# First batch's queries as seven block products, with the sums around them moved between engines

## The chip, the cores and the metric

The kernel runs on one core of one Trainium2 chip. The time is device microseconds from start to end of one execution; lower is better. Engines are named as in the profile: PE is TensorE (PEld its weight loads), DVE is VectorE, ACT is ScalarE, POOL is GpSimd, SP is SyncE, which only issues DMAs here.

## What is computed

Hidden states of 2 batches x 1,024 tokens x 512 are layer-normed to `xn`. Two things are made of `xn`, and the output joins them: single-head attention, and a mixture of 8 experts of which each token uses its best two.

```python
xn = layernorm(x)
q, k, v = split(xn @ w_qkv.T + b_qkv)                       # each (2, 1024, 512)
s = softmax(q @ k.T / sqrt(512)) @ v @ w_out.T + b_out
logits = xn @ router_w + router_b                           # 8 experts
w, idx = softmax(top_k(logits, 2))
h_e = silu(xn @ expert_w[e] + expert_b[e])
f = sum over the two experts of w * h_e
y = xn + f @ proj_w + proj_b
out = x + s * silu(norm_w * y / rms(y))
```

All data are float32.

## The kernel before, in words

Tokens are in 16 tiles of 128 (`NT`), 8 to a batch; the width of 512 is four chunks of 128 (`KC`). Every matmul of float32 shows as two records of the profile.

**Weights folded.** Wq and Wk are multiplied once into `wqk` (`product`, L583), and Wv and Wout into `rwvo` (`product_vo`, L407), so queries are `xn @ wqk + u` and values are ready to be summed as output. The biases enter through small sums: `weighted` (L320) is a weighted sum of four chunks of a weight on DVE, and `columns` (L331) turns it with four small matmuls against `ones`. `sq` (from the turned Wq and the bias of K) becomes column 8 of the router's weights `rw`, copied at L487; `sk` (from the turned Wk and the bias of Q) becomes `u`; `vb` (from Wout and the bias of V) is added to `bo` (L531, L532) and later to the values. `turn_w` (L132) turns Wq or Wk, four transposes on DVE.

**The order is that of the program.** `keep_order` (L71) ties every engine's instructions to the written order. So an instruction that waits holds all behind it on its engine; the same goes for the DMAs that an engine issues (SP, POOL and ACT issue DMAs here).

**First stage (L420 to L544).** For each tile, `parts` (L340, four `bn_stats` on DVE), `means` and `variances` (L353 and L368, for 2 or 4 tiles at once: a small matmul `pmean` or `pvar` on PE, then small instructions on DVE, among them three that write `dev` and one that writes `shift`, and a root on ACT), `norm` (L377, on ACT), `store` (L385, SP writes `xn` to DRAM), `turn_x` (L393, one transpose on DVE into `xnT`), and `value_half` (L457, PE: half of the tile's values and, in half 0, the router's logits). The loop over tiles t = 2 to 15 (L500) has these calls in a hand-made order: a tile's turn one step ahead of its product, its norm two ahead, means and variances of tiles 4, 8 and 12 at t = 2, 5 and 9. Between them stand: `bo`'s load on POOL (t = 2, L519), the turn of Wk (t = 8), `sk` (t = 9), `vb` (t = 10), `u` (t = 11), `pvb` (t = 12), which is the last user of the pool `raw`, and the 32 loads of the experts' weights `ew` into that pool's memory (t = 13, L535 to L542), half issued by SP, half by POOL. `eb`, the experts' biases (2 MB, L548), follows on SP.

**Routing and queries (L550 to L754).** DVE finds each token's experts and its place in a list sorted by expert, some 40 small instructions in a chain. PE needs its results at `pk` (L640), at the matmuls of `ptok` (L712, which take `lsel` and `tsel`) and at `pm` (L746). Between these PE does `product(0)` to `product(3)` and the first batch's queries: `queries(oc)` (L550), for each of four chunks of the outcome 2 halves x 4 chunks of the sum = 8 matmuls of 512 columns into a pair of banks (`ps_big`, two buffers), then one instruction of ACT adds `u` and writes `qT`. The memory of `qT` is that of the turned Wq and Wk, `wqkT`, until `product(3)` has read it.

**Experts (L757 to L867).** Tokens go by in `NS` = 39 slots of 128 rows. In a pipeline (L846), the slot's rows are fetched by an indirect DMA of POOL seven slots ahead (`gather`), written and read back in another order by SP (`put_s`, `take_s`), turned on DVE one slot ahead (`turn_s`), multiplied by the expert's weights on PE (`expert`, `ph`), given `eb` by DVE (L840) and SiLU by ACT, and written to DRAM. `pw` (the projection) is loaded at slot 8.

**Attention, combination, gate (L879 on).** The second half of the kernel works on pairs of tiles. It has block products by seven already: scores and attended values of pairs are made from seven products of half blocks with sums on DVE and POOL (`pair_scores`, `attend`).

Of the kernel before, what the change touches and what calls it, by code (L numbers as in the profile page):

```python
# [20 lines left out]
P = 128  # L21
# [6 lines left out]
def kernel(  # L28
# [200 lines left out]
    for q in range(4):  # L229
        for j in range(KC):  # L230
            gps.tensor_copy(bqk[ts(q, QP), :, j], bqkv[ts(j, QP), 0:2, q])  # L231
    spread(gps, wZ[0], w_qkvT[:, ts(0, H)], others)
# [6 lines left out]
    ln_eps = const.tile([P, 1], FP, name="ln_eps")  # L239
    gps.memset(ln_eps, LN_EPS)  # L240
    rms_eps = const.tile([P, 1], FP, name="rms_eps")
    gps.memset(rms_eps, RMS_EPS)
# [3 lines left out]
    ones = const.tile([P, P], FP, name="ones")  # L246
    gps.memset(ones, 1.0)

# [71 lines left out]
    def weighted(w_, bias, name):  # L320

        s_ = raw.tile([P, H], FP, tag="s", name=name, bufs=3)
        for c in range(KC):
            b_ = bias[:, c : c + 1]
            if c:
                dve.scalar_tensor_tensor(s_, w_[:, c, :], b_, s_, ALU.mult, ALU.add)
            else:
                dve.tensor_scalar(s_, w_[:, c, :], b_, None, ALU.mult)
            yield s_
# [120 lines left out]
    sum_q = weighted(wqkT[:, 0:KC], bqk[:, 1], "sq")  # L450
    next(sum_q)
    next(sum_q)
# [23 lines left out]
    value_half(0, 1)  # L476
    means(2, 2)
    next(sum_q)
    sq_ = next(sum_q)
    value_half(1, 1)  # L480
# [3 lines left out]
    pbb = ps_mm.tile([P, 512], FP, tag="mm", name="pbb")  # L484
    pe.matmul(pbb[:, 0:KC], lhsT=ones, rhs=bb, start=True, stop=True)
    dve.tensor_reduce(rb[:, E:E1], pbb[:, 0:KC], AX.X, ALU.add)
    dve.tensor_copy(rw[:, :, E], columns(sq_, "pw"))  # L487
# [12 lines left out]
    for t in range(2, NT):  # L500
# [14 lines left out]
        if 3 <= t < 7:  # L515
            parts(2 * t + 2)
            parts(2 * t + 3)
        if t == 2:
            gps.dma_start(bo, b_out.partition_broadcast(P))  # L519
        if t == 8:  # L520
            turn_w(wqkT[:, KC:], wZ[1])
        if t == 9:
            *_, sk_ = weighted(wqkT[:, KC:], bqk[:, 0], "sk")
        if t == 10:

            *_, vb = weighted(wo, bqkv[:, 2], "vb")
        if t == 11:
            dve.tensor_copy(u, columns(sk_, "pu"))
        if t == 12:
            pvb = ps_mm.tile([P, 512], FP, tag="mm", name="pvb")  # L530
            pe.matmul(pvb, lhsT=ones, rhs=vb, start=True, stop=True)  # L531
            dve.tensor_tensor(bo, pvb, bo, ALU.add)  # L532
            close(raw_guard)
        if t == 13:
            ew_guard, ewp = pool("ew", side="right")  # L535
            ew = ewp.tile([P, E, KC, H], FP, name="ew")
            for e in range(E):
                for q in range(4):
                    (sp if q in ours else gps).dma_start(  # L539
                        ew[ts(q, QP), e],  # L540
# [212 lines left out]
    for oc in range(2, KC):  # L753
        queries(oc)  # L754
# [608 lines left out]
```

## Time and profile before

| what | value |
|---|---|
| median of 3 runs | 541.28 us (538.69 to 543.67) |
| the profiled execution | 540.82 us |
| its span in the profile | 539.1 us |
| PE busy | 527.3 us (98%) |
| DVE busy | 311.2 us (58%) |
| POOL busy | 236.0 us (44%) |
| ACT busy | 167.0 us (31%) |
| first stage, PE's values from L487 on | from 32.0 us |
| queries of the first batch (L555) | from 105.6 us |
| first expert slot on PE | 134.5 us |
| first scores of attention on PE (L1057) | 256.1 us |

The profile is of one execution. Its page has the busy time of each engine, the span in 40 slices (the clock that PE was granted is one row), the chain of work that ended last, the costliest groups of instructions, and the DMA issues. A group's line gives line, engine, operation, what is written and read, and the count; then busy time in us and the mean of one in ns; then how long the engine sat idle before these and what ended it. A timeline's line gives start and length in us, engine, line, operation, count, and in brackets the idle time before it and its releaser. Where several like instructions follow each other they are merged, and the length is that of all.

### The profile page before, as it was taken

The page shows a single profiled execution, that of the slowest core. Times are in us where ns is not written, and L with a number is a line of the kernel's source. Part 1 is how long each engine was busy: PE and PEld are TensorE (multiplying, and loading weights), DVE is VectorE, ACT ScalarE, POOL GpSimd, SP SyncE. Part 2 cuts the span into 40 slices and gives each one's busy share as a digit, 9 for nine tenths or more (in the row PEclk, how much of TensorE's full clock was granted, in tenths as well). Part 3 has the DMA queues.
Part 4 walks back from the last instruction along what each step waited for, and adds up shares of the span by engine and source line. Part 5 has one row for each costly group of instructions (what it writes and reads, how often), then busy time and mean ns, then how long its engine had stood idle before and what let it go on. Part 6 is the DMA issues. An engine that isn't in the chain of part 4 may idle for free.

```text
span 539.1 us, 5950 instructions
## 1 busy us (share of the span) xinstructions
PE 527.3 (98%) x1762; PEld 322.1 (60%) x1762; DVE 311.2 (58%) x565; ACT 167.0 (31%) x316; POOL 236.0 (44%) x272
## 2 busy tenths in 40 slices
PE   7999999999999999999999999999999999999996
PEld 5778877444444444444466656756846657484585
DVE  2565652840333333333859376375697685949586
ACT  1535562211311111111333422423426234152340
POOL 8610006022234875230227445246189755464542
PEclk9989999999999999999999999999999999999999
DMA  9995339999999999994387922723625638295512
GB/s 212 206 220 127 78 79 227 275 217 336 319 338 331 359 348 338 318 290 146 125 281 234 299 83 92 273 78 123 229 78 179 230 95 297 71 312 176 187 54 78
DMA packets 89057, 112.37 MB, mean 208 GB/s; under 512 B 6849, under 2 KB 59201, under 8 KB 88897
## 3 DMA queue, kind: packets, MB, share of 16 engines
q1 hardware_dynamic: 75072, 75.51, 47.5%
q0 software_dynamic: 8192, 26.24, 16.4%
q10 hardware_dynamic: 5760, 10.23, 5.0%
q8 instruction: 15, 0.25, 0.2%
q14 instruction: 18, 0.14, 0.1%
HBM read 70.54 MB, written 41.42 MB: 208 GB/s over the span
## 4 chain that ended last, share of the span: by engine, by line
PE 87%; DVE 6%; issue 3%; DMA 2%; POOL 1%; ACT 1%; DVEq 0%; POOLq 0%
PE ph L814 20%; PE so L1147 17%; PE pp L1076 14%; PE po L1013 10%; PE pv L462 10%; PE pq L555 5%; PE pr L574 4%; PE sc L1057 3%; PE pqk L586 3%; DMA wZ<-in_L_attn_w_qkv_dram 2%; DVE sc L1082 1%; DVE pT L120 1%; ACT x L380 1%; POOL bqk L231 1%; DVE h L840 1%
## 5 line engine op out<-in xcount | busy, mean ns | idle before, releaser
L814 PE MATMUL ph<-ew,gT 128*128 x280 | 120.3, 592 | 0.0
L814 PEld LDWEIGHTS ph<-ew,gT 128*128 128x128 f32 x280 | 53.2, 190 | 66.9 <-issue 66.9
L788 POOL DMA_INDIRECT xg<-xn_d,tok x39 | 37.3, 957 | 78.2 <-DMA xs<-xg 52.2
L840 DVE TENSOR_TENSOR h<-ph,eb 128x512 f32<-128x512 f32 x39 | 26.8, 690 | 75.6 <-issue 40.4
L462 PE MATMUL pv<-rwvo,xnT 128*128 128x256 f32 (+1 forms) x256 | 60.9, 394 | 1.8 <-DVE xnT L120 1.0
L462 PEld LDWEIGHTS pv<-rwvo,xnT 128*128 128x128 f32 x256 | 48.6, 194 | 11.2 <-ACT x L380 1.4
L843 ACT ACTIVATE h<-h 128x512 f32<-128x512 f32 x39 | 24.5, 629 | 97.7 <-DVE h L840 89.0
L1013 PE MATMUL po<-pw,ct 128*128 128x512 f32 x112 | 49.2, 592 | 0.0
L975 POOL DMA_INDIRECT hg<-ho_d,posi_m x32 | 32.4, 1013 | 37.0 <-DVE nm L1041 23.4
L1044 ACT ACTIVATE pr<-sc,nm 128x1024 f32<-128x1024 f32 x16 | 18.3, 1145 | 90.7 <-DVE nm L1041 89.0
L1154 DVE TENSOR_TENSOR o<-so,o 128x256 f32<-128x256 f32 x49 | 20.0, 421 | 38.8 <-PE so L1147 25.9
L1192 POOL TENSOR_TENSOR o<-o,base 128x512 f32<-128x512 f32 x14 | 20.6, 1493 | 45.3 <-DVE o L1157 45.3
L1076 PE MATMUL pp<-xnT,qT 128*128 128x512 f32 x84 | 39.5, 592 | 0.0
L1147 PE MATMUL so<-vo,pT 128*128 128x256 f32 x168 | 38.5, 379 | 0.0
L1013 PEld LDWEIGHTS po<-pw,ct 128*128 128x128 f32 x112 | 21.3, 190 | 25.5 <-issue 25.3
L1147 PEld LDWEIGHTS so<-vo,pT 128*128 128x128 f32 x168 | 31.9, 190 | 7.3 <-issue 2.6
L120 DVE STREAM_TRANSPOSE gT<-sz 128x512 f32<-128x512 f32 x39 | 27.4, 702 | 13.4 <-DMA sz<-xs 13.4
L1082 DVE TENSOR_TENSOR sc<-pp,sc 128x512 f32<-128x512 f32 x49 | 31.6, 679 | 5.2 <-PE pp L1076 5.2
L539 POOL DMA_DIRECT2D ew<-in_L_ffn_expert_w_dram x16 | 8.7, 551 | 57.6 <-PE pvb L531 51.2
L574 PE MATMUL pr<-xnT,wqk 128*128 128x256 f32 x128 | 28.8, 381 | 0.9 <-DVE sc L1082 0.9
L120 DVE STREAM_TRANSPOSE pT<-pz 128x1024 f32<-128x1024 f32 x14 | 28.2, 2011 | 0.2 <-DMA pz<-ps 0.2
L574 PEld LDWEIGHTS pr<-xnT,wqk 128*128 128x128 f32 x128 | 24.2, 190 | 6.6 <-DVE sc L1082 2.2
(227 smaller groups left out, 819.9 us busy)
## 6 DMA issues: line engine op xcount, KB each, us to landing
xs<-xg SPq DMA_DIRECT2D x39, 256.0 KB, 4.7
sz<-xs SPq DMA_DIRECT2D x39, 256.0 KB, 4.6
ho_d<-h ACTq DMA_DIRECT2D x39, 256.0 KB, 4.7
ps<-pr SPq DMA_DIRECT2D x16, 512.0 KB, 3.3
pz<-ps SPq DMA_DIRECT2D x16, 512.0 KB, 5.7
xn_d<-x SPq DMA_DIRECT2D x32, 128.0 KB, 2.4
ew<-in_L_ffn_expert_w_dram POOLq DMA_DIRECT2D x16, 256.0 KB, 10.9
ew<-in_L_ffn_expert_w_dram SPq DMA_DIRECT2D x16, 256.0 KB, 13.6
```

The costliest lines, as they stand in the source:

```text
L120: dve.transpose(dst.rearrange(f"p j {order} -> p i j a", a=QP), z.rearrange("p i (j b) -> p i j b", b=QP),)
L462: pe.matmul(pvs[t][:, n, : HH + E1 * (1 - n)], lhsT=xnT[t // ST][:, c, ts(t % ST, P)], rhs=rwvo[:, c, cols], start=(c == 0), stop=(c == KC ...
L555: pe.matmul(ps[:, half, :], lhsT=wqk[:, c, ts(oc, P)], rhs=xnT[0][:, c, ts(half, 512)], start=(c == 0), stop=(c == KC - 1),)
L574: pe.matmul(ps[:, :PW], lhsT=wqk[:, c, ts(oc, P)], rhs=xnT[1][:, c, ts(k, PW)], start=(c == 0), stop=(c == KC - 1),)
L788: gps.indirect_dma_start(out=xg[s], out_offset=None, in_=xn_d, in_offset=bass.IndirectOffsetOnAxis(ap=tok[:, s : s + 1], axis=0),)
L814: pe.matmul(ph, lhsT=g_[:, c, :], rhs=ew[:, ds(r, 1), c, :].rearrange("p e f -> p (e f)"), start=(c == 0), stop=(c == KC - 1),)
L840: dve.tensor_tensor(h, ph, eb[:, ds(r, 1), :].rearrange("p e f -> p (e f)"), ALU.add)
L975: gps.indirect_dma_start(out=g_, out_offset=None, in_=ho_d, in_offset=bass.IndirectOffsetOnAxis(ap=posi_m[:, n, t : t + 1], axis=0),)
L1013: pe.matmul(po, lhsT=c_[:, c, :], rhs=pw[:, c, :], start=(c == 0), stop=(c == KC - 1))
L1076: pe.matmul(ps, lhsT=l_[:, c, :], rhs=r_[:, c, :], start=(c == 0), stop=(c == KH - 1))
L1082: dve.tensor_tensor(dst, ps, other, ALU.add)
L1147: pe.matmul(ps[:, :w_], lhsT=l_[:, c, :], rhs=r_[:, c, :], start=(c == 0), stop=(c == SK - 1),)
```

## The change

- Three memsets on POOL (`ln_eps`, `rms_eps`, `ones`) stand before the loads of Wq.
- `weighted` takes an engine and does all four chunks at once. `sq` stays on DVE and is finished before the first values. `sk` and `vb` go to POOL, where a chunk after the first is two instructions (a scaling into `m_`, a sum): seven in all each.
- `value_half(1, 1)` stands before `means(2, 2)`; `pbb` and the copy into `rw` before `variances(2, 2)`.
- In the loop: `parts` of tiles 12 and 13 at t = 6 and of 14 and 15 at t = 7 (before: 5 and 6); `vb` at t = 2 on POOL, after `bo`'s load; `pvb` at t = 4; Wk's turn and `sk` at t = 5; `u` and the end of `raw` at t = 8; the weights of expert e at t = 8 + e.
- The first batch's queries are `wqk` (2 x 2 blocks of 256 x 256) times `xnT[0]` (2 x 2 blocks of 256 x 512) by seven block products with 4 sums of each side's blocks. S1 to S4, of `wqk`, are made on DVE; T1 to T4, of `xnT[0]`, on POOL, T1 in the place of the outcome's block C22. The sums live in a new pool `qs`. The products' sums are made on DVE from PSUM, two instructions of 512 columns for each; `u` is added on the way. Products 1 and 4 stand before `ptok`, 6 after the routing, 7, 5 and 3 after `pm`. Product 2 stands at slot 0 of the experts; ACT copies it to `pw`'s memory and POOL adds it to C11.
- `eb` is loaded after `qs` has been closed, into its place, issued by ACT.

The core of the diff:

```diff
-    def weighted(w_, bias, name):
+    def weighted(w_, bias, name, eng):
         s_ = raw.tile([P, H], FP, tag="s", name=name, bufs=3)
         for c in range(KC):
             b_ = bias[:, c : c + 1]
             if c:
-                dve.scalar_tensor_tensor(s_, w_[:, c, :], b_, s_, ALU.mult, ALU.add)
+                if eng is dve:
+                    dve.scalar_tensor_tensor(s_, w_[:, c, :], b_, s_, ALU.mult, ALU.add)
+                else:
+                    m_ = raw.tile([P, H], FP, tag="m", name=f"{name}_m{c}", bufs=2)
+                    eng.tensor_scalar(m_, w_[:, c, :], b_, None, ALU.mult)
+                    eng.tensor_tensor(s_, s_, m_, ALU.add)
             else:
-                dve.tensor_scalar(s_, w_[:, c, :], b_, None, ALU.mult)
-            yield s_
+                eng.tensor_scalar(s_, w_[:, c, :], b_, None, ALU.mult)
+        return s_
...
-    sum_q = weighted(wqkT[:, 0:KC], bqk[:, 1], "sq")
-    next(sum_q)
-    next(sum_q)
+    sq_ = weighted(wqkT[:, 0:KC], bqk[:, 1], "sq", dve)
...
     value_half(0, 1)
+    value_half(1, 1)
     means(2, 2)
-    next(sum_q)
-    sq_ = next(sum_q)
-    value_half(1, 1)
+    pbb = ps_mm.tile([P, 512], FP, tag="mm", name="pbb")
+    pe.matmul(pbb[:, 0:KC], lhsT=ones, rhs=bb, start=True, stop=True)
+    dve.tensor_copy(rw[:, :, E], columns(sq_, "pw"))
     variances(2, 2)
...
-        if 3 <= t < 7:
-            parts(2 * t + 2)
-            parts(2 * t + 3)
+        if t in (3, 4, 6, 7):
+            first = {3: 8, 4: 10, 6: 12, 7: 14}[t]
+            parts(first)
+            parts(first + 1)
         if t == 2:
             gps.dma_start(bo, b_out.partition_broadcast(P))
-        if t == 8:
-            turn_w(wqkT[:, KC:], wZ[1])
-        if t == 9:
-            *_, sk_ = weighted(wqkT[:, KC:], bqk[:, 0], "sk")
-        if t == 10:
-            *_, vb = weighted(wo, bqkv[:, 2], "vb")
-        if t == 11:
-            dve.tensor_copy(u, columns(sk_, "pu"))
-        if t == 12:
+            vb = weighted(wo, bqkv[:, 2], "vb", gps)
+        if t == 4:
             pvb = ps_mm.tile([P, 512], FP, tag="mm", name="pvb")
             pe.matmul(pvb, lhsT=ones, rhs=vb, start=True, stop=True)
             dve.tensor_tensor(bo, pvb, bo, ALU.add)
+        if t == 5:
+            turn_w(wqkT[:, KC:], wZ[1])
+            sk_ = weighted(wqkT[:, KC:], bqk[:, 0], "sk", gps)
+        if t == 8:
+            dve.tensor_copy(u, columns(sk_, "pu"))
             close(raw_guard)
-        if t == 13:
             ew_guard, ewp = pool("ew", side="right")
             ew = ewp.tile([P, E, KC, H], FP, name="ew")
-            for e in range(E):
...
+        if 0 <= t - 8 < E:
+            e = t - 8
+            for q in range(4):
+                (sp if q in ours else gps).dma_start(
...
-    eb_guard, ebp = pool("eb", side="right")
-    eb = ebp.tile([P, E, H], FP, name="eb")
-    sp.dma_start(eb, expert_b.partition_broadcast(P))
-
-    def queries(oc):
...
+    def times(banks, l_, r_):
+        for o in range(2):
+            for c in range(KH):
+                pe.matmul(
+                    banks[o], lhsT=l_[:, c, ts(o, P)], rhs=r_[:, c],
+                    start=(c == 0), stop=(c == KH - 1),
+                )
+        return banks
...
+    def query_products():
+        p1 = times(big(1), A11, B11)
+        for o in range(2):
+            act.copy(C11[:, o], p1[o].rearrange("p (k f) -> p k f", k=2))
+        p4 = times(mm(4), A22, T4)
+        yield
+        dve.tensor_tensor(S1, A21, A22, ALU.add)
+        dve.tensor_tensor(S2, S1, A11, ALU.subtract)
+        yield
+        dve.tensor_tensor(S3, A11, A21, ALU.subtract)
+        dve.tensor_tensor(S4, A12, S2, ALU.subtract)
+        plus(C12, times(big(6), S2, T2), C11)
+        yield
+        plus(C21, times(big(7), S3, T3), C12)
+        p5 = times(big(5), S1, T1)
+        plus(C22, p5, C21, 1)
+        plus(C12, p5, C12)
+        plus(C21, p4, C21, 1)
+        plus(C12, times(big(3), S4, B22), C12, 0)
+        yield
+
+    def last_query_product(place):
+        p2 = times(big(2), A12, B21)
+        for o in range(2):
+            act.activation(place[:, o], p2[o], AF.Identity, bias=u[:, o : o + 1])
+        gps.tensor_tensor(C11, C11, by_pairs(place), ALU.add)
+
+    gps.tensor_tensor(T3, B22, B12, ALU.subtract)
+    gps.tensor_tensor(T2, T3, B11, ALU.add)
+    gps.tensor_tensor(T4, B21, T2, ALU.subtract)
...
     product(2)
     product(3)
-    queries(0)
+    gps.tensor_tensor(
+        T1, *(b.rearrange("p o (k f) -> p o k f", k=2) for b in (B12, B11)), ALU.subtract
+    )
+    pq = query_products()
+    next(pq)
...
+    next(pq)
     tk = rt.tile([P, 2, NSP], FP, name="tk")
...
-    queries(1)
+    next(pq)
     pm = ps_mm.tile([P, 512], FP, tag="mm", name="pm")
...
-    for oc in range(2, KC):
-        queries(oc)
+    next(pq)
+    close(qs_guard)
+    eb_guard, ebp = pool("eb", side="right")
+    eb = ebp.tile([P, E, H], FP, name="eb")
+    act.dma_start(eb, expert_b.partition_broadcast(P))
...
     for s in range(-steps[0][1], NS):
+        if s == 0:
+            last_query_product(pw[:, 0:2])
         pipeline(steps, s, NS)
```

## The prediction

> **What bounds the kernel now.** I read the page, then the chain of work that ended last, then the timelines of the stages the diff touches, then groups by shape and DMA issues.
>
> ```profile
> span 539.1 us, 5950 instructions
> ...
> PE 527.3 (98%) x1762; PEld 322.1 (60%) x1762; DVE 311.2 (58%) x565; ACT 167.0 (31%) x316; POOL 236.0 (44%) x272
> ...
> PE 87%; DVE 6%; issue 3%; DMA 2%; POOL 1%; ACT 1%; DVEq 0%; POOLq 0%
> ```
>
> TensorE (PE) is busy 98% of the span and 87% of the chain. So an edit counts by what it takes from PE, or by what it makes PE wait for; DVE, ACT and POOL only count where PE waits for them. The chain in order of time (start, length, what) from the queries on:
>
> ```profile
> 105.78 6.87 PE pq L555 x16
> 112.65 1.15 PE ptok L712 x32
> 113.80 6.94 PE pq L555 x16
> 120.74 0.17 PE pm L746 x2
> 120.91 13.79 PE pq L555 x32
> 134.69 109.88 PE ph L814 x256
> ```
>
> Sixteen matmuls of 512 columns take 6.87 us, 0.429 each, back to back through the queries (L555) into the experts (L814): this stretch is priced by counting matmuls. PE's few waits have to be found in the timelines.
>
> **The products (gain).** A logical fp32 product is two records (32 logical in queries, 64 records). Seven block products of 2 x 2 logical are 56 records, so 8 x 0.429 = **-3.43 us**, certain as long as nothing around them waits. Checked from the end of the token matmuls (113.8): p6, then pm, p7, p5, p3, p2 are 3.43 + 0.17 + 4 x 3.43, so ph begins at 131.2 instead of 134.7. DVE has 12 sums from PSUM of 128x512 (L1082 takes 679 ns for one) and four between SBUF tiles (half of L928's 1.22 for 1,024 columns). After p5 ends (124.3) it has eight of them, 5.6 to 6.1 us, then the first turn of gathered rows, 0.70: 131.1 at the latest. p2, placed last and summed by POOL, is the cover: 3.43 us without which ph would wait about 3.4. gT(0)'s data are there: before, gather to turn took 17 us (115.2 to 132.2) beside eb and the last of ew; both are gone from this stretch. S1 and S2 end at 113.2, before DVE needs ptok at 113.8: tok is not late. POOL's C11 sum waits for p2 and delays gather 7 to about 135, whose ph comes at 155: hidden by the 20 us of lead.
>
> **Wk's sums off DVE (gain).** sk and vb (2 x 2.8 us of DVE at L326/L328) leave DVE; before, they stood ahead of a turn that PE waited for (71.81 below): **-0.99**. `pu` and `pvb` only change places on PE; the last `parts` at t = 7 still precede pmean at t = 9.
>
> **The values' bias on POOL (loss).** vb now follows bo's issue on POOL, whose order is fixed. The timeline there:
>
> ```profile
> 28.51 0.18 DVE L357 TENSOR_TENSOR dev<-st,mean 128x16 f32<-128x16 f32 x1
> ...
> 29.39 0.57 POOL L519 DMA_DIRECT2D bo<-in_L_attn_b_out_dram  x1 [0.72 <-DMA x<-_attn_hidden_states_dram]
> ...
> 31.32 0.17 DVE L373 SCALAR_TENSOR_TENSOR shift<-mean,rstd 128x8 f32<-128x8 f32 x1
> ...
> 35.98 1.60 DVE L342 BATCH_NORM_STATS2 st<-x 128x6 f32<-128x128 f32 x8
> ...
> 39.02 0.31 PE L348 MATMUL pmean<-st,eighth 128*128 128x32 f32 x2
> ```
>
> So vb starts at about 30.0 and is seven instructions long. In the changed order DVE does all of sq (ends 29.9), then means(2,2), whose three `dev` instructions read two SBUF tiles, and only then the copy of the router's column for which PE's v(0,0) waits (before: 32.0). The row that decides is from the attention stage (start, length of both, count at the end):
>
> ```profile
> 318.71 2.95 POOL L1006 TENSOR_TENSOR xr<-xr,pb 128x512 f32<-128x512 f32 x2
> ...
> 318.76 3.45 DVE L989 SCALAR_TENSOR_TENSOR hg<-hg,wgt_m,hg 128x512 f32<-128x512 f32 x2
> ```
>
> Alone, L989 takes 743 ns (its minimum); beside two POOL sums two take 3.45, 1.73 each: one full POOL instruction is waited for each time. The Trainium skill, "SBUF — State Buffer", section "Who interferes with whom", says the same and more, that a DVE instruction with two SBUF inputs is blocked entirely while a GpSimd instruction reads SBUF, whatever its length. The row shows this for 512 columns only. By the row alone one could scale the wait with DVE's own length (0.17 x 1.3: four short ones lose 0.9); by the rule each waits out one POOL instruction. I take the rule. POOL's prices:
>
> ```profile
> L965 POOL TENSOR_TENSOR sp<-pT 128x512 f32<-128x512 f32 x7 | 8.9, 1273 | 34.3 <-DVE pT L120 34.3
> ...
> L915 POOL TENSOR_TENSOR sw<-qT 128x256 f32<-128x256 f32 x7 | 5.1, 727 | 6.3 <-DMA xs<-xg 6.3
> ...
> L299 POOL TENSOR_SCALAR mix<-mixed,number 128x128 f32<-128x128 f32 x1 | 0.6, 622 | 0.1
> ```
>
> A sum of 512 columns is 1.27. A scaling (tensor_scalar) is not shown at this width: L299 is 0.62 for 128 columns and L225 0.32 for 32, which continues to 1.81; the skill's "GPSIMD Engine Reference", section "Elementwise — side-by-side cycle accounting", has 769 ns as the best for 512 elements of one input, an estimate of 0.97 with the 0.2 of a 32-column copy (L227). No run here shows that. I take 1.3, between, since L299 compares and L225 is mostly fixed cost. Then dev ends at 30.0 + 1.3 + 1.3 + 1.27 + 3 x 0.2 = 34.5, v(0,0) starts at 34.8; pvar, std, rstd and a blocked `shift` put norm(2) at 36.6 (before 31.5); from there DVE's order is fixed, norm and turn 2.4, two `parts`, turn, two `parts` (1.6, 0.7, 1.6): 42.9, when PE can do pmean of tiles 4 to 7 (before 39.0). **+3.9**. Ends: with no blocking sq's earlier end makes it 38.4, **-0.6**; with scalings of 1.81, +5.6. PE's clock (granted 0.50 from 32 to 35.3 in the windows, after the thin stretch before it) may stay low longer, but PE would then still reach pmean by about 42.3: covered. The earlier ln_eps gives nothing: std gains 1.16, but DVE then waits for wZ until 21.85 all the same.
>
> **Wk turned at t = 5 (loss).** DVE after the variances of tile 8, PE's wait behind sk, and the last instruction ahead of pk:
>
> ```profile
> 53.68 1.64 DVE L342 BATCH_NORM_STATS2 st<-x 128x6 f32<-128x128 f32 x8
> ...
> 55.24 0.69 DVE L120 STREAM_TRANSPOSE xnT<-x 128x512 f32<-128x512 f32 x1
> ...
> 71.81 3.75 PE L462 MATMUL pv<-rwvo,xnT 128*128 128x256 f32 x16 [0.99 <-DVE xnT L120]
> ...
> 97.08 0.29 DVE L636 TENSOR_TENSOR before<-upto,both 128x128 f32<-128x128 f32 x1
> ```
>
> turn_w (2.45) takes the place of 1.64 of `parts`, so tile 7's turn ends at 56.9 where PE wants it at 56.2: **+0.75** (0 to 0.9). Then sk on POOL: 4 x 1.3 + 3 x 1.27 + gaps 0.4 = 9.4 from 56.5 is 65.9, plus the wake, and PE comes to `pu` at 64.75: **+1.3** (0 with scalings of 0.97, +3.6 with 1.81). Behind `pu` on PE stands the whole rest.
>
> **Expert weights from t = 8, and the sums of inputs on POOL (loss).** ew's 32 issues (16 of 0.31 on SP, 16 of 0.55 on POOL) cost PE nothing by themselves: POOL is idle there, and SP's stand between stores that only the gathers at 115 read. But T3, T2, T4 and T1 have 1,024 columns: from 256 to 512 columns 0.55 more, so 2.37 each. T3 waits for the tile x, whose memory qt takes over (by the tiles' sizes in the pools' order), hence for the last store of x, now issued on SP behind expert weights (SP: ew of experts 3 and 4 stand before it). If it lands 2.4 us after its issue as before, the three run at 86 to 93 and DVE's routing (from 92.1, nearly all two-input) is hardly touched. If it waits for the backlog (7.5 MB asked by then in 18 us, some 4.7 delivered at the 260 GB/s of the windows at 84 to 104), it lands at about 93 and all three stand in DVE's way, 7.1 us. The slack: `before` ends at 97.37 and PE reads it at 98.25, 0.88. T1 (after product(3), 105.8) always meets tsel and lsel: 2.37 less the 1.56 that the last lsel is early. So 0.8 + (0 to 6.2): **+3.5**, the middle, one to two of the three in the way.
>
> **Experts' biases later (loss or nothing).**
>
> ```profile
> eb<-in_L_ffn_expert_b_dram SPq DMA_DIRECT2D x1, 2048.0 KB, 15.2
> ```
>
> Now issued by ACT (0.35; behind it p2's copy, not due before 131) once p3 has read qw (127.8), eb must land before h(0) and turn(2) on DVE, which ph(2) needs at 138.0: both take 1.4, so within 8.8 us. Before, it took 15.2 behind 1 MB of ew and beside four gathers, and 2 MB at the 360 to 420 GB/s seen at 120 to 126 would be 5 to 6 and some 2 for latency. Beside puts and takes I expect 10.3: **+1.5** (0 to 5). Behind h(0) on DVE stand the turns, and PE behind these.
>
> **Sum.** -3.43 - 0.99 + 3.9 + 0.75 + 1.3 + 3.5 + 1.5 = +6.5, on the profiled execution's 540.8 (span 539.1 and 1.7 around it): 547.3. The median of the runs lies 0.5 above that execution; **547.5**.
>
> **Rivals.** (1) *The short instructions slip through.* If DVE's instructions of 0.17 to 0.3 us are not held up, the front gives -0.6 in place of +3.9 and the routing 0: -1.5 in all, **539.8**. It speaks for this that the only rows of blocking are of 0.74; against it, that the wait shown there is POOL's length. It decides when `dev` stays at 0.17 to 0.20. (2) *Half of it:* x's last store lands early, or vb starts too late to meet `dev`[...]: 3 to 4 less, **543.5**. (3) *eb is late:* at 200 GB/s, the rate of 112 to 120, 10.5 + 2 and contention make 5, and PE's clock falls in the gap (half of 3.3 us): **553**. (4) *The seven products wait for each other* (DVE's sums hold the two big banks): by the times above p5's bank frees 0.4 before p2 asks; three late sums would give back 2 of the 3.4. It is in the range of all the cases.
>
> **How the numbers follow.** A measurement of this kernel tells about 1% (5.4 us) from no change; its runs spread 0.9%. Forecast 0.45 (544 to 552; 0.38 of it above 546.7, 0.07 below), half 0.25 (0.05 slower, 0.20 same), slipping through 0.22 (with no sk wait and eb hidden 537, and with a front clock that no longer falls 535.3: 0.17 same, 0.05 faster), eb late 0.08 (slower). So faster 0.05, same 0.44, slower 0.51. Range 538.5 to 553.5, leaving out the best of the third and most of the last; the forecast's own is 544 to 552.
>
> **What would show it.** In the new profile: 56 query matmuls and ph starting 17.4 us after ptok; `dev` (L357 to L364) of tiles 2, 3 at a microsecond or more each, v(0,0) near 34.8; PE idle at `pu` before POOL's sk; DVE's routing instructions at 2 us beside T3 to T4; h(0) waiting for eb's DMA. Were `dev` at 0.2 and PE without a gap before pk, the forecast is wrong at its first step.

## The result and the profile after

| | median | runs |
|---|---|---|
| before, measured beside it | 540.42 us | 6, 538.69 to 543.67 |
| changed | 553.74 us | 6, 552.78 to 556.87 |
| ratio | 1.0261 | 95% interval 1.0235 to 1.0287 |

The change costs 13.3 us by the medians. The execution with the profile took 556.74 (span 555.0), one of two of the six that lie 3 us above the other four; what sets these two apart is not settled. Against the profiled span before (539.1) it is 15.9 longer. Four starts on PE, read from the two timelines, show where:

| starts at (us) | before | after | its part of the difference |
|---|---|---|---|
| `product(0)`, behind all values | 91.2 | 96.2 | +5.0 |
| first query product | 105.6 | 110.6 | 0 |
| first expert slot | 134.5 | 143.9 | +4.4 |
| first scores of attention | 255.9 | 271.9 | +6.6 |

From there to the end the two run alike (283.2 and 283.1). PE's waits in the timeline of the changed kernel (start, length, line, in brackets the idle time before and its releaser), where the kernel before, from 41 us to the scores, had only one of 0.99 at 71.81 and one of 0.19 just ahead of the scores:

```profile
57.16 5.05 PE L464 MATMUL pv<-rwvo,xnT 128*128 128x256 f32 x22 [0.70 <-ACT x L384]
...
66.80 1.46 PE L339 MATMUL pu<-ones,sk 128*128 128x1 f32 x8 [2.37 <-POOL sk L330]
...
110.61 3.60 PE L573 MATMUL pq<-xnT,wqk 128*128 128x512 f32 x8
118.42 5.40 PE L573 MATMUL pq<-qt,wqk 128*128 128x512 f32 x8 [4.22 <-POOL qt L628]
...
126.39 3.70 PE L573 MATMUL pq<-qt,qw 128*128 128x512 f32 x8 [0.86 <-DVE qw L606]
...
155.52 4.97 PE L883 MATMUL ph<-ew,gT 128*128 x7 [4.61 <-DVE gT L120]
```

Three things are late: `sk` for `pu`, the third sum of columns (T4) for p4 (the product at 118.42; p1, at 110.61, has no wait), and the rows of slot 2. Behind each of the long waits the clock falls. The stretches of the same trace (times, then busy us of PE, PEld, DVE, ACT, POOL with counts, the granted clock, DMA share, GB/s):

```profile
67.00:74.00 7.00, 7.00 (x23) 5.86 (x23) 1.56 (x6) 0.00 (x0) 4.42 (x8) 0.52 0.68 155
...
118.00:124.00 6.00, 5.58 (x18) 2.50 (x19) 6.00 (x4) 0.00 (x0) 3.65 (x2) 0.72 0.01 3
...
155.00:160.00 5.00, 4.48 (x7) 1.94 (x8) 1.75 (x3) 0.63 (x1) 2.84 (x3) 0.66 1.14 363
```

PE is busy in all 7 us of the first stretch, at half its clock (granted 0.52): the two halves behind `pu` took 3.76 and 3.09 where 1.9 and 2.0 are usual. The wait of 2.37 at `pu`, `pu` itself (1.46, before 0.95) and these 2.9 make +5.8 at this place; with the turn's 0.70, the stall that is gone (-0.99) and a front that is 0.7 sooner, this is 4.8 of the +5.0 in the table. Likewise p4's eight matmuls took 5.40 in place of p1's 3.60. With p4's wait of 4.22 and those at ptok (0.38) and for S2 (0.86) that is 7.3; the table has 7.8, its +4.4 and the 3.43 that the eighth product had taken. Slot 2 waits 4.61 and loses some 2 to the clock (granted 0.66 behind it), the +6.6.

**The sums.** SP's queue (start, length), where the stores of x stand between the weights' loads:

```profile
89.85 6.05 SPq L392 DMA_DIRECT2D xn_d<-x  x4
96.41 3.64 SPq L538 DMA_DIRECT2D ew<-in_L_ffn_expert_w_dram  x4
100.17 1.95 SPq L392 DMA_DIRECT2D xn_d<-x  x4
```

Before, SP issued the last store by 84.5. Here it goes out at 102 and lands at 107.4, as SP's issues are held back by earlier transfers (how, is told at slot 2). T3 starts at once behind it, and meets the widest instructions of the routing. POOL, then DVE:

```profile
107.60 3.67 POOL L626 TENSOR_TENSOR qt<-xnT 128x1024 f32<-128x1024 f32 x1 [23.62 <-DMA xn_d<-x]
```

```profile
109.10 7.07 DVE L752 TENSOR_TENSOR tsel<-hsel,tpart 128x1280 bf16<-128x1280 bf16 x2
116.10 8.91 DVE L769 TENSOR_TENSOR lsel<-mixed,lo 128x1024 bf16<-128x1024 f32 x4
```

The same two on DVE in the kernel before, and a POOL sum of this size with DVE idle in the changed one (C11's):

```profile
104.35 2.90 DVE L691 TENSOR_TENSOR tsel<-hsel,tpart 128x1280 bf16<-128x1280 bf16 x2
107.16 4.62 DVE L704 TENSOR_TENSOR lsel<-mixed,lo 128x1024 bf16<-128x1024 f32 x4
```

```profile
145.49 2.35 POOL L624 TENSOR_TENSOR qT<-qT,pw 128x1024 f32<-128x1024 f32 x1 [5.49 <-ACT pw L623]
```

Both sides lose: a sum takes 3.3 to 3.7 in place of 2.35, `tsel` 7.07 in place of 2.90, `lsel` 8.91 in place of 4.62.

**Slot 2.** SP's waits, and the turn on DVE that PE waits for:

```profile
SPq L116 <- DMA eb<-in_L_ffn_expert_b_dram: 10.3, 1, 10.3
```

```profile
154.75 0.71 DVE L120 STREAM_TRANSPOSE gT<-sz 128x512 f32<-128x512 f32 x1 [3.13 <-DMA sz<-xs]
```

A take of sorted rows (L116) reads nothing of `eb`, yet SP holds it for the 10 us of that load. The built program tells why: the transfers issued by SP and ACT take eight semaphores in turn, and the third take has the one of `eb`, so it may go out only when `eb` has landed. In the same way an issue of SP stands behind the transfer eight before it, which is how the weights' loads hold up the stores.

### The profile page after: what moved, and what is told of

Same layout as the page of the kernel before. It is cut to its first block, busy times and chain, and to the rows that moved or that the text cites. A ratio compares the mean times of both kernels' runs of the same rounds, so it can differ in the third digit from the quotient of the medians.

```text
span 555.0 us, 5967 instructions
## 1 busy us (share of the span) xinstructions
PE 530.5 (96%) x1754; PEld 323.7 (58%) x1754; DVE 325.6 (59%) x573; ACT 165.0 (30%) x316; POOL 272.0 (49%) x291
## 4 chain that ended last, share of the span: by engine, by line
PE 72%; DVE 10%; DMA 10%; issue 3%; POOL 2%; SPq 2%; ACT 1%; DVEq 0%; ACTq 0%; POOLq 0%
PE ph L883 19%; PE so L1217 17%; PE pp L1146 13%; PE po L1083 10%; PE pr L635 4%; PE pv L464 3%; DMA ew<-in_L_ffn_expert_w_dram 3%; DMA wZ<-in_L_attn_w_qkv_dram 3%; PE pq L573 3%; PE sc L1127 2%; DMA eb<-in_L_ffn_expert_b_dram 2%; DVE lsel L769 2%; DVE tsel L752 1%; DMA xn_d<-x 1%; DVE st L346 1%
## 5 line engine op out<-in xcount | busy, mean ns | idle before, releaser
L883 PE MATMUL ph<-ew,gT 128*128 x280 | 122.3, 599 | 4.6 <-DVE gT L120 4.6
L464 PE MATMUL pv<-rwvo,xnT 128*128 128x256 f32 (+1 forms) x256 | 62.1, 399 | 1.9 <-ACT lg L476 1.1
L1114 ACT ACTIVATE pr<-sc,nm 128x1024 f32<-128x1024 f32 x16 | 18.3, 1144 | 90.9 <-DVE nm L1111 89.1
L1083 PEld LDWEIGHTS po<-pw,ct 128*128 128x128 f32 x112 | 21.3, 190 | 25.5 <-issue 25.3
L120 DVE STREAM_TRANSPOSE gT<-sz 128x512 f32<-128x512 f32 x39 | 27.2, 700 | 3.2 <-DMA sz<-xs 3.1
L120 DVE STREAM_TRANSPOSE pT<-pz 128x1024 f32<-128x1024 f32 x14 | 28.1, 2007 | 0.0
L1059 DVE SCALAR_TENSOR_TENSOR hg<-hg,wgt_m,hg 128x512 f32<-128x512 f32 x16 | 24.3, 1554 | 4.4 <-ACT hg L1055 4.4
## 6 DMA issues: line engine op xcount, KB each, us to landing
xn_d<-x SPq DMA_DIRECT2D x32, 128.0 KB, 5.7
ew<-in_L_ffn_expert_w_dram POOLq DMA_DIRECT2D x16, 256.0 KB, 10.3
```

What stands on the lines that cost most here:

```text
L120: dve.transpose(dst.rearrange(f"p j {order} -> p i j a", a=QP), z.rearrange("p i (j b) -> p i j b", b=QP),)
L464: pe.matmul(pvs[t][:, n, : HH + E1 * (1 - n)], lhsT=xnT[t // ST][:, c, ts(t % ST, P)], rhs=rwvo[:, c, cols], start=(c == 0), stop=(c == KC ...
L883: pe.matmul(ph, lhsT=g_[:, c, :], rhs=ew[:, ds(r, 1), c, :].rearrange("p e f -> p (e f)"), start=(c == 0), stop=(c == KC - 1),)
L1083: pe.matmul(po, lhsT=c_[:, c, :], rhs=pw[:, c, :], start=(c == 0), stop=(c == KC - 1))
```

## The experiments

All kernels below are the changed one but for the edit shown, unless said otherwise. The starts on PE are those of one profiled execution each; up to the first it differs by 2 us and more between kernels with the same code there (before 91.2; before without eb 89.1), so the later columns, which are lengths, say more.

| kernel | median | ratio to before | `product(0)` at | to p1 | p1 to slot 0 | slot 0 to scores |
|---|---|---|---|---|---|---|
| before | 540.4 | | 91.2 | 14.4 | 28.9 | 121.4 |
| changed | 553.7 | 1.0235 to 1.0287 | 96.2 | 14.4 | 33.3 | 128.0 |
| e1 weights behind stores | 553.8 | 1.0192 to 1.0286 | 95.7 | 22.4 | 25.5 | 126.5 |
| e2 `u` a step later | 550.4 | 1.0163 to 1.0202 | 88.8 | 14.4 | 33.7 | 128.8 |
| e3 eb issued by POOL | 553.0 | 1.0169 to 1.0255 | 97.1 | 14.4 | 33.2 | 124.8 |
| e4 e1 to e3 together | 546.0 | 1.0087 to 1.0121 | 91.2 | 15.4 | 32.1 | 124.4 |
| e5 sums on DVE, late place | 564.6 | 1.0392 to 1.0470 | 95.3 | 33.5 | 25.5 | 128.5 |
| e6 eb sooner, routing's place | 553.9 | 1.0230 to 1.0291 | 95.0 | 14.4 | 35.4 | 121.5 |
| e7 e1, e2, e5, e6 together | 554.8 | 1.0248 to 1.0300 | 88.9 | 26.1 | 30.4 | 124.5 |
| e8 e7 with eight products | 541.4 | 1.0007 to 1.0035 | 89.1 | 14.4 | 28.9 | 121.4 |
| e9 sums on DVE in its idle time | 549.7 | 1.0108 to 1.0221 | 96.6 | 14.4 | 26.0 | 127.1 |
| e10 eb sooner, sums' place | 552.1 | 1.0176 to 1.0266 | 95.3 | 14.4 | 35.3 | 121.5 |
| e11 e1, e2, e9, e10 together | 540.0 | 0.9981 to 1.0015 | 91.7 | 14.4 | 28.1 | 121.6 |
| e12 e11, sums on POOL | 539.3 | 0.9977 to 1.0007 | 89.8 | 14.4 | 28.9 | 123.2 |
| e13 e11 without eb | 535.3 | 0.9890 to 0.9929 | 88.8 | 14.4 | 25.5 | 121.7 |
| e14 e11, eb ahead of gathers | 539.8 | 0.9984 to 1.0008 | 89.3 | 14.4 | 27.5 | 123.6 |
| e15 e11, weights between stores | 539.4 | 0.9979 to 1.0004 | 89.0 | 14.4 | 28.4 | 121.5 |
| e16 before without eb | 540.5 | 1.0000 to 1.0021 | 89.1 | 14.4 | 28.9 | 121.4 |

### One late thing at a time: e1 to e4

```diff
# e1
-        if 0 <= t - 8 < E:
-            e = t - 8
+        if t == 13:
+            for e in range(E):
# e2 (the weights' loads a step later as well)
-        if t == 8:
+        if t == 9:
             dve.tensor_copy(u, columns(sk_, "pu"))
# e3
-    act.dma_start(eb, expert_b.partition_broadcast(P))
...
         if s == 0:
+            gps.dma_start(eb, expert_b.partition_broadcast(P))
             last_query_product(pw[:, 0:2])
```

> The changed kernel, but the 32 loads of the experts' weights are issued together at t = 13, behind the stores of x, and no longer from t = 8 between them. Theory (the stores of x stand on SP's queue behind the weights' loads, so the sums of columns on POOL start at 107.6 us and TensorE waits 4.2 us for the third of them): the last store lands some 6 us earlier, the wait for the third sum and the low clock behind it go, and about 7.8 us come back: some 546 us. Rival (the sums on POOL and VectorE's selections slow each other down wherever they run together, and the queue has little to do with it): some 2 us come back, 551 us or more.

Measured: 553.8, no gain: the rival's number. The sums did start 10 us sooner, at 97.3, but now among the routing's short instructions. DVE, then PE:

```profile
97.27 2.47 DVE L669 TENSOR_TENSOR key<-lg,m 128x128 f32<-128x128 f32 x1
99.85 2.32 DVE L670 TENSOR_TENSOR key<-key,order 128x128 f32<-128x128 f32 x1
...
102.53 2.07 DVE L675 TENSOR_TENSOR hot<-key,km 128x128 f32<-128x128 f32 x1
```

```profile
107.53 0.59 PE L701 MATMUL pk<-upto,ones 128*128 128x8 f32 x2 [4.84 <-DVE upto L695]
```

Each of these takes 0.29 alone. POOL's three sums (2.35 each) hold one DVE instruction each for nearly their whole length, and the wait moves from p4 to `pk`. The queue was not the cause by itself.

> The changed kernel, but u is taken from pu one step later (t = 9 in place of 8), with the weights' loads one step later too and two experts' loads at t = 15. TensorE should no longer wait 2.4 us for sk. Theory (the last store of x still lands near 107 us, so TensorE only waits longer for the third sum of columns; two waits in a row are not added): about the same, 552 to 554 us. Rival (each wait and the low clock behind it is lost for itself): 5.8 us come back, some 548 us.

Measured: 550.4, 3.3 less. PE no longer waits at `pu`, and `product(0)` starts 7 us sooner in the profile (the medians show half of it; how much clock the wait at `pu` costs differs from run to run, as e5 shows). The last store landed sooner too, near 100, so that p4's wait for T4 stayed as it was (4.61). The number lies between the two theories: the loss at `pu` is at least in part one of its own, since SP and POOL reach the later steps sooner when PE does.

> The changed kernel, but eb's load is issued by POOL and not by ACT, at the start of slot 0. Theory (SP's third take of sorted rows waits for eb's load because the hardware queues' transfers share eight semaphores in turn, and the one that it needs is eb's): the take no longer waits, slot 2's products start where they did before, and some 3 us come back (the wait of 4.6 us, less what VectorE may still wait for eb's data): about 550.6 us. Rival (what counts is only when eb's data land, 10 us after the issue): no change, 553.7 us.

Measured: 553.0, within the scatter of these runs (their intervals overlap). SP's wait for eb is gone, and DVE waits for eb's data in its place:

```profile
153.47 0.69 DVE L908 TENSOR_TENSOR h<-ph,eb 128x512 f32<-128x512 f32 x1 [8.92 <-DMA eb<-in_L_ffn_expert_b_dram]
```

The turns stand behind `h` on DVE, so slot 2 waits 3.10 in place of 4.61. The semaphore is the first of two locks on the same door; the load has to land sooner.

> The three edits together: the weights' loads behind the stores of x, u one step later, eb's load from POOL. Theory: the three losses are those of the order in which loads, sk and eb are issued, and not of the seven products; they come back together, 7.8 + 5.8 + 3.1 us, which gives some 537 us, a little under the kernel before (540.4). Rival (the sums on POOL cost VectorE and TensorE time of their own, whatever the loads do): 543 to 547 us.

Measured: 546.0, 7.8 less than the changed kernel but 5.5 above the kernel before, as the rival said. What is left shows on DVE, where two of the instructions are:

```profile
97.07 2.30 DVE L697 TENSOR_TENSOR before<-upto,both 128x128 f32<-128x128 f32 x1
...
99.48 2.19 DVE L709 TENSOR_SCALAR cnt<-cnt 128x8 int32<-128x8 int32 x1
```

Four instructions of 0.17 to 0.29 take 2.2 to 2.3, one for each of T3, T2, T4 and T1, 8 us of the routing's chain. PE then waits for `lsel` four times (2.8 in all), the clock is at 0.50 from 116 to 122, and slot 2 waits 2.76, as DVE's `h` waits for eb.

### The sums elsewhere: e5 to e8

e5 gives the four sums to DVE, ahead of the sum of the logits, for which it waits 8 us anyway. e6 loads `eb` into the place that the routing leaves, before the seventh product. e7 has both with the edits of e1 and e2; e8 is e7 with `queries(oc)` of the kernel before.

```diff
# e5: x in two tiles, of which the first half is dead by t = 7
+    x_ = [
+        xap.tile([P, ST, 4, P], FP, name="xa"),
+        ln.tile([P, ST, 4, P], FP, name="xb"),
+    ]
...
-    gps.tensor_tensor(T3, B22, B12, ALU.subtract)
-    gps.tensor_tensor(T2, T3, B11, ALU.add)
-    gps.tensor_tensor(T4, B21, T2, ALU.subtract)
+    dve.tensor_tensor(T3, B22, B12, ALU.subtract)
+    dve.tensor_tensor(T2, T3, B11, ALU.add)
+    dve.tensor_tensor(T4, B21, T2, ALU.subtract)
+    dve.tensor_tensor(T1, B12, B11, ALU.subtract)
     dve.tensor_tensor(lg1, lg1, rb.unsqueeze(1).to_broadcast([P, NT, E1]), ALU.add)
# e6: pw and eb on the left, behind close(rc_guard) and before next(pq)
-    eb_guard, ebp = pool("eb", side="right")
+    eb_guard, ebp = pool("eb")
```

> The changed kernel, with the four sums of columns (T1 to T4) made by VectorE in the 8 us in which it waits for the last logits, in a space whose last user is the first half of x (its stores are long done then), and no longer by POOL beside VectorE's routing; u, the weights' loads and eb's load stay as in the changed kernel. Theory (POOL's two-input sums and VectorE's instructions hold each other up, and TensorE waits for the third sum): the wait for the third sum, the wait of ptok and the low clock behind them go, 7.8 us: 546 us; TensorE goes through the queries without a wait. Rival (the loss is the late stores of x): nothing is won, 552 us or more, for the stores are as late as before.

Measured: 564.6, on the rival's side and far above its 552. My layout failed its purpose: `qt` came to lie over the second half of x as well, so DVE stood before its first sum until the last store had landed, and with it the whole routing:

```profile
109.34 1.22 DVE L564 TENSOR_TENSOR qt<-xnT 128x1024 f32<-128x1024 f32 x1 [21.42 <-DMA ew<-in_L_ffn_expert_w_dram]
```

(The releaser named is the transfer that ended last; in the built program the instruction waits for the stores of the second half of x.) It shows the price of the late stores where the waiting engine is not POOL: 16.77 us of PE's waiting at `pk`. And it shows that a sum is 1.22 on DVE.

The run shows one thing more. It has the changed kernel's wait at `pu`, for the same `sk`, and the clock behind it does not fall:

```profile
69.29 1.05 PE L350 MATMUL pu<-ones,sk 128*128 128x1 f32 x8 [2.38 <-POOL sk L341]
```

```profile
69.00:76.00 7.00, 6.71 (x37) 6.01 (x38) 2.17 (x9) 1.41 (x5) 4.65 (x9) 1.00 0.69 155
```

Seven of the profiled executions have this wait (2.37 to 2.39, then the same eight matmuls). Read in windows of half a us, the clock is low for 6.6 to 6.8 us behind it in four of them (changed, e3, e6, e10), for 3.4 in two (e1, e9) and not at all here. So the same wait costs 2.4 to 5.8 us, and one profile shows only one of these prices. The 3 us between the executions of the changed kernel are of this size; that they come from it is not shown.

> The changed kernel, with eb's load issued some 16 us sooner (behind the second batch of query products, in the place that the routing leaves, in front of the seventh product). Theory (both eb's data and the take that shares its semaphore are late by the 10 us that the load takes): the wait of 4.6 us at slot 2 and the low clock behind it go, 6 us: some 547 to 548 us. Rival (POOL's late gathers bound slot 2 anyway): 551 us or more.

Measured: 553.9, no gain in the median, though slot 0 to scores is 121.5 again. Slot 2's wait is gone, but with `eb` in that place the gathers' buffers lie over the sums: the second gather waits for p7 (133.7, 5.8 us behind the first), and PE waits 1.64 for slot 0's rows. The rival's number, by my layout.

> The weights' loads behind the stores of x, u one step later, the sums of columns by VectorE in its idle time and eb's load early. Theory: nothing of the three losses is left, and the gain of seven products (3.4 us) stands with the stall of 1 us that went at t = 10: 536 us, 0.8% under the kernel before. Rival (products that feed each other through VectorE and POOL cannot follow one another without waits): 540 us or more.

Measured: 554.8. Both faults of e5 and e6 in one kernel; POOL's second gather waits for p5 to have read its sums:

```profile
133.97 0.99 POOL L866 DMA_INDIRECT xg<-xn_d,tok  x1 [6.34 <-PE pq L588]
```

> The same as the run with everything mended, but the queries of the first batch by eight products as in the kernel before, without the sums. Theory: 3.4 us above that run (the eighth product), some 539.5 us. Rival (the saved product is lost again in the sums and in waits): no difference to that run.

Measured: 541.4. Not comparable to e7, whose waits come from the sums' space that e8 lacks. It is worth something else: Wk's turn, `vb` and `sk` on POOL and the weights' order, with `u` at t = 9 and no sums, are nearly level with the kernel before (0.2% above it, ratio 1.0007 to 1.0035). So what e7 loses beyond comes with the seven products and their space.

### The layouts mended: e9 to e12

```diff
# e9: the S sums below, the T sums at the top, over the first half of x only; T1 behind S4
+    qw = qs.tile([P, 4, KH, 2 * P], FP, name="qw")
     qt = qs.tile([P, 3, KH, 512], FP, name="qt")
# e10: what p3 and p5 read is put outside eb's place
+    qw14 = qs.tile([P, 2, KH, 2 * P], FP, name="qw14")
+    qw23 = qs.tile([P, 2, KH, 2 * P], FP, name="qw23")
     qt = qs.tile([P, 3, KH, 512], FP, name="qt")
```

> The changed kernel with the sums of columns T3, T2, T4 made by VectorE before the logits' sum, as in the run before, but in a place whose only earlier user is the first half of x, so that they need not wait for the last stores of x; T1 is made by VectorE behind S4. u, the weights' loads and eb's load stay as in the changed kernel. Theory (the late sums and their meeting with VectorE's routing cost 7.8 us, and both go): the sums run at 88 to 93 us, the first products follow each other without a wait, 546 us. Rival (they only lay bare the next wait, the gathers behind the late stores of x): 550 us or more.

Measured: 549.7, 4.0 less. p1 to slot 0 falls from 33.3 to 26.0, and PE's only wait there is 0.36 for S2: the stage's loss is gone, 7.2 us in the profile. The median shows about half and lies near the rival's bound; the waits at other places remain (0.70 for the turn, 2.38 at `pu`, 3.72 at slot 2).

> The changed kernel with the sums' space laid out so that eb's load has to wait for the seventh product (S3, T3) and no longer for the third (S4): it is issued some 7 us sooner. The gathers' space is as in the changed kernel. Theory (eb's data and the semaphore that it shares with SP's third take come too late): slot 2's wait of 4.6 us and the low clock behind it go, 547 to 548 us. Rival: another wait of the slots takes the place, 551 us or more.

Measured: 552.1. Slot 0 to scores is back at 121.5, but slot 0 itself now waits 2.17: eb's load, issued at 132.6, runs while the first rows are fetched (sixth gather at 136.7, seventh at 144.3).

> Both of these, the weights' loads behind the stores of x, and u one step later. Theory: the losses are all gone and one product is saved against the run with eight products (541.4): 538 us. Rival (a wait between the seven products or at the slots remains): 541 us or more.

Measured: 540.0, the kernel before to within 0.2%, and 1.4 under e8 where a product is 3.4. PE passes from p1 to p2 without a wait; the sums sit at 84 to 88 on DVE. Most of the saved product is then lost at the first slot:

```profile
134.18 46.25 PE L894 MATMUL ph<-ew,gT 128*128 x107 [2.45 <-DVE gT L120]
```

> As the run before, but T3, T2 and T4 are made by POOL at the same place. Theory (POOL's sums cost only where VectorE works beside them; here it is idle until 92 us, and they end by then or a little later): within 1.5 us of the run before. Rival (sums on POOL cost in any place): 4 us or more above it.

Measured: 539.3, no different from e11. POOL's sums, 2.35 each, end at 91.2, when one instruction of the routing has begun (held for 0.4). POOL's last sum and that instruction (0.31 in e11):

```profile
88.86 2.35 POOL L567 TENSOR_TENSOR qt<-xnT,qt 128x1024 f32<-128x1024 f32 x1
```

```profile
90.70 0.67 DVE L568 TENSOR_TENSOR lg<-lg,rb 128x144 f32<-128x144 f32 x1 [8.30 <-ACT lg L487]
```

So not the engine but the company was dear: the same three instructions on the same engine held DVE for 6 of e4's 8 us, and for 0.4 here.

### Where the saved product goes: e13 to e16

In e11 the transfers nearly rest from 115 to 117 (DMA share 0.27); eb's 2 MB are issued at 121.5 and take 10.6 us, just when the rows of the first slots go out and come back. SP's waits there:

```profile
SPq L112 <- DMA xg<-xn_d,tok: 20.8, 8, 9.2
...
SPq L116 <- DMA xs<-xg: 6.7, 3, 5.9
```

e13 is e11's kernel and e16 the kernel before, both without the experts' biases: their load is left out and `bo` is added in their place, so the outcome is another one. e14 is e11's kernel with the load placed ahead of the gathers:

```diff
# e13, e16
-    eb = ebp.tile([P, E, H], FP, name="eb")
-    act.dma_start(eb, expert_b.partition_broadcast(P))
...
-            h, ph, eb[:, ds(r, 1), :].rearrange("p e f -> p (e f)"), ALU.add
+            h, ph, bo, ALU.add
# e14: T2 and T4 in pw's place, T3 made a second time, S1 to S4 in lsel's
+            qt = pwp.tile([P, KC, H], FP, tag="pw", name="qt")
...
+    sp.dma_start(eb, expert_b.partition_broadcast(P))
+    qs_guard, qs = pool("qs", side="right")
```

> The mended kernel (sums by VectorE in its idle time) without eb's load: the experts' biases are left out, and b_out's sum bo is added in their place, so that VectorE's instruction stays. Theory (eb's 2 MB beside the first gathers cost slot 0 its 2.5 us): 537 us, 3 us under the mended kernel (540.0). Rival (the chain from the tokens to slot 0 is too long for seven products): 540 us.

Measured: 535.3 (0.989 to 0.993), and slot 0 starts right behind p2:

```profile
128.66 51.53 PE L891 MATMUL ph<-ew,gT 128*128 x119
```

From p1 to slot 0 it is 25.48, 3.43 under the 28.91 of the kernel before: the product, to the last digit. The median is 4.7 under e11's; 2.6 of this is in the stretch from p1 to slot 0, and where the rest lies is not shown.

> The mended kernel with the space laid out anew, so that eb's load is issued right behind the weights' loads and before the first gather, as in the kernel before: T2 and T4 lie in the place of the projection's weights (T3 is made a second time in T4's place, 1.2 us of VectorE), the S sums in the place of lsel. The computation is whole. Theory (as in the run before): slot 0 no longer waits, 537 to 538 us, 0.5% under the kernel before. Rival: 540 us.

Measured: 539.8, the rival's number, though with other waits than the rival's. Slot 0 has no wait, but the stretch from p1 to it is only 0.6 shorter than in e11 (27.5 and 28.1): p6 and p7 wait 0.78 and 0.83 for S2 and for the second T3, which this layout makes late. Two later slots wait 0.86 and 0.80 for their rows. From 160 to 250 us the DMA share is 0.97 here, 0.98 in the kernel before and 0.99 in e11; that an earlier start only reaches this limit sooner is argued, not shown.

> The mended kernel (540.0 us) with the weights' loads between the stores of x again, as the changed kernel has them, one step later (from t = 9, two experts at t = 15). Theory (the late stores cost only through the sums that waited for them; the gathers start at 115 us, 8 us behind the last store): 540 us, no difference. Rival (the late stores and the fuller queue hold the gathers as well): 542 us or more.

Measured: 539.4, no difference. Weights read between the stores cost nothing by themselves.

> The kernel before without eb's load: the experts' biases are left out, and b_out's sum bo is added in their place. Theory (there eb's load lies in front of the gathers, where the queues are nearly empty, and TensorE waits for nothing at the slots): no difference, 540 us, so that the whole 4.8 us of the mended kernel without eb are those of seven products and of the stall that went. Rival (eb's 2 MB cost the kernel before as well): 537 us or less.

Measured: 540.5, no gain. But the reason expected is not the one that the traces show. In the kernel before, eb is issued ahead of the first gather (111.8 and 115.2) and yet in flight until 127, beside the first four; the DMA share from 112 to 128 is 1.04. The first turn of gathered rows comes late for it too, as the kernel before and then e16 show:

```profile
132.15 0.71 DVE L120 STREAM_TRANSPOSE gT<-sz 128x512 f32<-128x512 f32 x1 [10.92 <-DMA sz<-xs]
```

```profile
124.81 0.71 DVE L120 STREAM_TRANSPOSE gT<-sz 128x512 f32<-128x512 f32 x1 [5.67 <-DMA sz<-xs]
```

Counted from p1, the rows are turned 27.2 us behind it with the load and 22.0 without. PE comes to slot 0 after 28.9 with eight products and 25.5 with seven. So eight products hide the load by 1.7 us, and seven do not; in e8, where eb was issued at 119.0, the rows were turned only 0.2 ahead of PE. By these times, as an estimate, a product saved with the load beside the gathers can show 1.7 of its 3.4 at most, and 0.2 in e8's order.

The medians of e16 and e13 are 5.1 us apart, of which 3.43 are the product's. Where the rest lies is not shown: the profiled executions of the two differ by 3.6 in all.

## Why the prediction was wrong

The sign was right; 553.7 was measured where 547.5 was forecast. The profiled execution is 15.9 longer than before. Its parts beside the terms of the forecast:

| term | forecast | in the profile |
|---|---|---|
| eighth product gone | -3.43 | -3.43 |
| stall at t = 10 gone | -0.99 | -0.99 |
| `vb` on POOL (the front) | +3.9 | -0.7 |
| Wk's turn at t = 5 | +0.75 | +0.70 |
| `sk` late at `pu` | +1.3 | +5.8 |
| sums of columns, late store | +3.5 | +7.8 |
| eb late | +1.5 | +6.6 |
| sum | +6.5 | +15.8 |

The step that failed is the pricing of three waits, `pu`, the sums and eb: together 13.9 too low. About half of this, 7.2, is the low clock behind the waits (3.4 at and behind `pu`, 1.8 at p4, some 2 at slot 2), which the three terms put at nothing. The other 6.7 are the waits themselves. The front was 4.6 too high the other way and hid a third of the miss, which is luck.

- **The products:** right, to 0.01 us. The stretch from p1 to slot 0 is 25.48 wherever PE does not wait in it (e1, e5, e13); in the changed kernel more is lost beside them.
- **The front, `vb` on POOL:** wrong in its mechanism. The failed step is "I take the rule": that each of `dev` and `shift` waits out one POOL instruction. DVE, then POOL, in the changed kernel:

```profile
29.52 0.72 DVE L361 TENSOR_TENSOR dev<-st,mean 128x16 f32<-128x16 f32 x1
30.27 0.17 DVE L367 TENSOR_TENSOR dev<-dev 128x16 f32<-128x16 f32 x1
...
38.91 0.90 DVE L361 TENSOR_TENSOR dev<-st,mean 128x32 f32<-128x32 f32 x1
```

```profile
29.51 1.58 POOL L332 TENSOR_SCALAR vb<-wo,bqkv 128x512 f32<-128x512 f32 x1
...
38.49 1.26 POOL L330 TENSOR_TENSOR vb<-vb,vb_m 128x512 f32<-128x512 f32 x1
```

The first `dev` was held for 0.55, the two behind it not at all, while the scaling ran on to 31.09; v(0,0) started at 30.95, not at 34.8. Only the two-input sum held `dev` to its own end (39.8). The rule, in the Trainium skill's "SBUF — State Buffer", "Who interferes with whom", speaks of any GpSimd instruction that reads SBUF; this trace bears it out for sums, not for scalings with one tensor. The row that the forecast rested on had two sums on POOL, and showed waits of 1.0 (1.73 less 0.74), not of a whole sum (1.27). The front came out 0.7 sooner: the lower end I had put (-0.6), for the reason given under the first rival.

- **`sk` late at `pu`:** the wait was foreseen, its price was not. A scaling takes 1.56, not 1.3, which makes the wait 2.37; and behind the wait stands a halved clock, which I had priced for eb and for the front but not here.
- **The sums of columns:** the cause was right, the path was not. I let the store land at 93 if it "waits for the backlog"; it landed at 107.4. The bytes were counted, but not that SP, in order, waits for earlier transfers before it issues the next. So the three sums met not the short instructions ahead of `pk` (that is e1) but `tsel` and `lsel`, where both sides slow down. PE did not wait at `pk`; it waited for T4 itself, ahead of p4. The middle of the forecast's own 0.8 to 7.0 would have been 3.9.
- **eb:** the load took 10.07 where I had 10.3, and yet slot 2 lost 6.6. The step that failed is "within 8.8 us": it looked for what reads eb (`h`), not for what waits behind its semaphore (SP's third take, and with it the turn). Rival 3 had the size (5 and the clock) with DVE as the waiting engine, which e3 shows to be the second lock.

The losses are not independent: e2, e9 and e10 alone bring 3.3, 4.0 and 1.6, their sum with e1's nothing 8.9, all together (e11) 13.8.

## What to carry to other kernels

When a product is saved by sums, ask where the sums' operands, their memory and their neighbours are: here the sums cost 8 us beside the routing and nothing where DVE had no work, on either engine; and the space that they took put off a 2 MB load from 6 us behind the first product to 15 or 30. When PE is to come sooner to a stage, ask also what else that stage needs: the rows of the first slots were ready 1.7 us ahead of PE, less than the 3.4 saved. A wait for memory names tiles that the computation never mentions, so list for each new tile who had its place before and when the last transfer out of it lands. And price a wait of PE with what follows it: three waits of 2.4 to 4.6 us cost 1.4 to 2.4 times their length, though the shortest of them cost no more than itself in another run (e5).

## What the runs showed of the hardware

- POOL's scaling of 128x512 (one tensor and a column) takes 1.55 to 1.58, more than its two-tensor sum of the same size (1.27). A sum of 1,024 columns is 2.35 alone and 3.3 to 3.7 beside DVE's wide two-tensor instructions; DVE's sum of that size is 1.22.
- In e1 and e4 each two-tensor sum of POOL that met short DVE instructions made one of them last 2.1 to 2.5 us, also one-tensor ones on integers (`cnt`, 2.19) and on 32 columns (`hi`, 2.27, both in e4); a reduction passes (`km`, 0.29 in e1).
- A wait of PE can halve its clock for some us, and its length alone does not decide. In the profiled executions, from 41 us to the scores, the clock stayed at 1.00 behind single waits of up to 2.17 (five of 0.42 to 1.25 close together, in e4, brought it down); behind those of 2.37 to 3.10 it fell in seven cases and stayed in five; from 3.17 on it fell in all. The kind of matmul behind the wait does not decide it either: `pu`'s eight of one column had both outcomes (e5 above), and so had eight and more of 512 columns behind 2.45. e10 and e11 (e11's is the line at slot 0 above):

```profile
115.75 5.40 PE L574 MATMUL pq<-qt,wqk 128*128 128x512 f32 x8 [2.45 <-POOL qt L629]
```

In e10 the eight took 5.40 in place of 3.60; in e11 the clock stayed at 1.00 from 134 to 141. What decides between the two is open.
